# Two more second-layer products in quarters, their ends summed in PSUM

## The chip, the cores and the metric

The kernel runs on one core of a Trainium2 chip. The metric is the device time of one execution in microseconds (us), as a median over runs.

## The reference

Everything is f32. Four layers follow one another; the change lies in the third, and in the second layer's feed-forward part, which shares its code.

```python
x = _L0_cond_ref(x, A_grid, B_grid, dt)        # finite differences on a 512x512 grid, cut to 8 batches in the kernel
# _L1: attention block, then
h = _ln(x) * g2 + beta2                        # x: (8, 512, 512) in the kernel
ff = _gelu2(h @ W1 + b1) @ W2 + b2             # W1: 512x2048, W2: 2048x512
x = x + ff
# _L2: an expert of 8 is chosen for each batch
h = gelu(x @ Wi[e] + bi[e])                    # Wi: 512x2048
o = h @ Wo[e] + bo[e]                          # Wo: 2048x512
r = o + x
y = (r - mean(r)) * rsqrt(var(r) + 1e-12) * gamma[e] + beta[e]
# _L3: a gate from the mean over the rows, and a low-rank response
x = y + strength * (((y @ basis) @ basis.T[:, :R]) @ resp_w.T + resp_b + safety_bias)
```

## The kernel before

The grid stage and the attention stage fill the first 1079 us and are not touched. Then `mlp_stage` runs sixteen **phases** q = 0 to 15, one per batch and layer: q = 0 to 7 are the feed-forward part of _L1 for the 8 batches, q = 8 to 15 the expert layer of _L2. Phases 9 to 15 also finish the batch of the phase before (`tail_norm`, `tail_normed`, `tail_gamma`, `tail_feats`, `gate`, `strength`, `add_beta`, `tail_sum`, `tail_add`: the layer norm and _L3), and phases 0 to 7 also hold the Gram-Schmidt steps (`gs_norm`, `gs_b`) for _L3's basis.

One phase multiplies 512x512 by 512x2048 (first layer) and 512x2048 by 2048x512 (second layer). Both products are done with seven instead of eight half-size products (Winograd's form of Strassen's scheme, in which sums S of the left operand and T of the right one are formed first, and the seven results are added up):

- First layer: in four column groups g = 0 to 3, seven products each (list `L1`), of four matmuls 128x128 by 128x256. The left sums S come from the weights `wi` (`w_quads`, on GpSimd, written POOL), the right sums T from the normalised and transposed input b (`b_quads`, on VectorE, written DVE). Tiles u in PSUM hold the products, DVE adds them up into `act`, and ScalarE (ACT) applies gelu in place.
- Second layer: seven products p1, p5, p2, p6, p3, p7, p4 in this order. `second` computes one as 16 matmuls of 128x256 into one PSUM tile y. `third` computes one as again seven quarter products of 128x128 blocks (28 matmuls of 128x128, with sums by `quarters`), into two PSUM tiles "a" and "b" that DVE adds up in an SBUF tile w. p7 and p4 use `third`; p1, p5, p2, p6 and p3 use `second`. In phase 15, p4 is done in two halves (`last_row`), so that the end of the run is short.

The order is written out by hand. `pin` keeps every instruction in program order on its engine, and the work of the other engines is placed by **steps** (hooks): `at(hooks, s, f)` runs f before step s of the phase. Steps 0 to 27 are the first layer's products, 28 to 31 p1, 32 to 35 p5, 36 to 39 p2, 40 to 43 p6, 44 to 47 p3, 48 to 51 p7, 52 to 55 p4; a step is a product of the first layer, a column group of a second-layer product, or seven quarter matmuls.

Names that the change and the prediction use:

- `add` (line 1217) is a two-operand DVE instruction, `gadd` (line 1220) one on POOL, `mm` (line 1211) a matmul. `stage` (line 1569) copies an operand to PSUM by ScalarE, in one of two buffers ("tr"), so that a DVE sum has one operand in PSUM and one in SBUF. Products live in six PSUM buffers ("u").
- `t13`, `t2s2`, `t4s4`, `s13`: the sums T1, T3, T2, T4 (POOL) and S1, S3, S2, S4 (DVE) of the second layer.
- `x_add` adds a product into one quadrant of x; `yu` holds a sum of p1 and p6.
- `rows32` transposes blocks of the next phase's input, `turn` and `spread` send them through DRAM to the transposed tile bt; `scale` (phases 0 to 6) applies g2 and beta2 to it.
- `load_wi(q, g)` loads 1 MB of weights into buffer x0 to x3 (tag `x{g}`). Buffers x1 to x3 of a phase serve the sums of the quarter products once its weights are used; x0 does not.
- `load_extra` loads the expert's bias, gamma and beta rows. DMAs are issued on SyncE's queue (SP).

Of the kernel before, what the change touches and what calls it, by code (L numbers as in the profile page):

```python
# [20 lines left out]
NB = 8  # L21
# [1176 lines left out]
def mlp_stage(tc, a, small, xp, io, wo8, x1d, ident, eidx, sigs, layernorm, rstd_of, phalf, wl3, g2, b1, first):  # L1198
# [4 lines left out]
    with ExitStack() as ctx:  # L1203
# [293 lines left out]

        def b_quads(q, hold=False):
            def b(i, k, j):
                v = bts[q][2 * i + k]  # L1500
                return v[:, 2 * j : 2 * j + 2, :, :] if len(v.shape) == 4 else v[:, H * j : H * j + H]

            t1, t2, t4 = (
                as_rows(ap.tile([P, 2, H], F32, name=f"tb{i}_{q}", tag=f"tb{i}", bufs=1), b(0, 0, 0))
                for i in range(3)
            )
            for k in range(2):
                add(t1[k], b(0, k, 1), b(0, k, 0), ALU.subtract)
                add(t2[k], b(1, k, 1), t1[k], ALU.subtract)

            def rest():
                for k in range(2):
                    add(b(0, k, 1), b(1, k, 1), b(0, k, 1), ALU.subtract)
                for k in range(2):
                    add(t4[k], b(1, k, 0), t2[k], ALU.subtract)

            if not hold:
                rest()
            tbs[q] = {
                "B00": lambda k: b(0, k, 0), "B10": lambda k: b(1, k, 0),  # L1520
                "B11": lambda k: b(1, k, 1), "T3": lambda k: b(0, k, 1),
                "T1": lambda k: t1[k], "T2": lambda k: t2[k],
                "T4": lambda k: t4[k],
            }
            return rest
# [26 lines left out]
        def run(q, hooks):  # L1552
# [13 lines left out]
            def stage(key, src):  # L1566

                t = ps.tile([P, src.shape[1], src.shape[2]], F32, name=f"st_{q}_{key}", tag="tr")
                pin(nc.scalar.copy(t, src))  # L1569
                st[key] = t  # L1570
# [3 lines left out]
            def s13(g):  # L1574
                t = st.pop(f"s13_{g}")
                ss[g] = io.tile([P, 2, H], F32, name=f"s_{q}_{g}", tag=f"v{g}", bufs=2)
                add(ss[g], t, act_quad(g, 1, 1))
                add(act_quad(g, 1, 0), act_quad(g, 0, 0), t, ALU.subtract)

# [52 lines left out]
            wo, ts = wos[q], {}  # L1632
            tvs = extra["t", q]

            def second(s, A, B, each=None):
                y = ps.tile([P, 2, H], F32, name=f"y_{q}_{s}", tag="u", bufs=6)
                for g in range(NG):
                    go(s + g)
                    if s == 28 and g == 1:
                        stage(f"s13_{NG - 1}", act_quad(NG - 1, 1, 0))  # L1640
                    if s == 28 and g == 2:
                        s13(NG - 1)
                    for i in range(2):
                        for m in range(2):
                            mm(
                                y[:, m, :], A(g)[:, i, m * P : (m + 1) * P], B(g)[:, i, :],
                                g + i + m == 0, g + i + m == NG + 1,
                            )
                    if each:
                        each(g)  # L1650
                return y

            def quarters(key, i, j, wi_, wj, homes):


                def left(k, m):
                    o = H * i + P * m
                    return acts[:, :, 2 * j + k, o : o + P]

                def right(k, n):  # L1660
                    o = H * wj + P * n
                    return wo[:, :, 2 * wi_ + k, o : o + P]

                s1, s2, s4, t1, t2, t4 = homes
                L, M = left, right
                four[key] = dict(
                    a=((L(0, 0), M(0, 0)), (s2, t2), (L(0, 1), M(0, 1)), (s1, t1)),
                    b=((L(1, 0), M(1, 0)), (s4, M(1, 1)), (L(1, 1), t4)),
                )
                sub = ALU.subtract  # L1670
                of_left = [
                    lambda: (stage(key + "a", L(0, 1)), stage(key + "b", L(0, 0))),
                    lambda: (
                        add(s1, st[key + "a"], L(1, 1)),
                        add(L(0, 1), L(0, 0), st[key + "a"], sub),
                        stage(key + "c", L(1, 0)),
                    ),
                    lambda: (add(s2, s1, st[key + "b"], sub), add(s4, st[key + "c"], s2, sub)),
                ]
                of_right = [  # L1680
                    lambda: gadd(t1, M(0, 1), M(0, 0), sub), lambda: gadd(M(0, 1), M(1, 1), M(0, 1), sub),
                    lambda: gadd(t2, M(1, 1), t1, sub), lambda: gadd(t4, M(1, 0), t2, sub),
                ]
                return of_left, of_right

            four = {}
            homes = {}

            def quarter_homes(n):
                for k in range(1, 4)[n:]:  # L1690
                    t = xp.tile([P, KC, D], F32, name=f"q4_{q}_{k}", tag=f"x{k}", bufs=1)
                    homes[k] = [t[:, c, :].rearrange("p (g d) -> p g d", g=NG) for c in range(KC)]

            def third(s, key):

                jobs = [
                    (n, k, g, v) for n in "ab" for k, v in enumerate(four[key][n]) for g in range(NG)
                ]
# [4 lines left out]
                y = ys["a"]  # L1703
                for i, (n, k, g, (A, B)) in enumerate(jobs):
                    if i % 7 == 0:
                        go(s + i // 7)
                    last = len(four[key][n]) - 1
# [9 lines left out]
                add(w[:, 0:3, :], ys["b"][:, 0:3, :], w[:, 0:3, :])  # L1717
                return w.rearrange("p (m n) d -> p m (n d)", m=2)

            def early_quarters():  # L1720
                quarter_homes(0)
                h1, h2, h3 = (homes[k] for k in (1, 2, 3))
                return (
                    quarters("p7", 1, 0, 0, 1, (h1[3], h2[0], h2[1], h1[0], h1[1], h1[2]))
                    + quarters("p4", 1, 1, 1, 0, (h3[1], h3[2], h3[3], h2[2], h2[3], h3[0]))
                )
# [10 lines left out]
            def t2s2(g):  # L1737
                if g < NG - 1:
                    stage(f"s2_{g + 1}", act_quad(g + 1, 0, 0))
                else:  # L1740
                    stage("s4_0", act_quad(0, 0, 1))
                gadd(tvs[g], quad(wo[:, g], 1, 1), tvs[g], ALU.subtract)
                add(ss[g], ss[g], st[f"s2_{g}"], ALU.subtract)

            def t4s4(g):
                if g < NG - 1:
                    stage(f"s4_{g + 1}", act_quad(g + 1, 0, 1))
                gadd(quad(wo[:, g], 1, 0), quad(wo[:, g], 1, 0), tvs[g], ALU.subtract)
                add(act_quad(g, 0, 1), st[f"s4_{g}"], ss[g], ALU.subtract)

            l7, r7, l4, r4 = early_quarters()
            for i, f in enumerate(r7):
                at(hooks, 28 + i, f)
            for i, f in enumerate(l7):
                at(hooks, 40 + i, f)
            if q < NQ - 1:
                for i, f in enumerate(l4):
                    at(hooks, 43 + 2 * i, f)
                for i, f in enumerate(r4):
                    at(hooks, 41 + i if q <= NB else 40, f)  # L1760
# [4 lines left out]
            p5 = second(32, lambda g: ss[g], lambda g: tvs[g], t2s2)  # L1765
            x_add(1, 1, p5)
            x_add(0, 1, p5)
            p2 = second(36, lambda g: act_quad(g, 0, 1), b(1, 0), t4s4)
            x_add(0, 0, p2)
            p6 = second(40, lambda g: ss[g], lambda g: tvs[g])  # L1770
            add(yu, p6, yu)
            x_add(0, 1, yu)
            p3 = second(44, lambda g: act_quad(g, 0, 1), b(1, 1))
            x_add(0, 1, p3)
            p7 = third(48, "p7")
            add(yu, p7, yu)
            x_add(1, 1, yu)
            x_add(1, 0, yu)
# [3 lines left out]
            else:  # L1782
                for m in range(2):
                    y = ps.tile([P, H], F32, name=f"y_{q}_52_{m}", tag="u", bufs=6)
                    for g in range(NG):
                        if g % 2 == 0:
                            go(52 + 2 * m + g // 2)
                        for i in range(2):
                            mm(
                                y, act_quad(g, 1, 1)[:, i, m * P : (m + 1) * P],  # L1790
                                b(1, 0)(g)[:, i, :], g + i == 0, g + i == NG,
                            )
                    last_row(m, y)

        def t13(q, g):
# [4 lines left out]
            extra.setdefault(("t", q), {})[g] = t  # L1800
# [23 lines left out]
        def tail_normed(q):  # L1824
            v, (mv, rs) = stats.pop(q)
            for r in range(len(v)):
# [6 lines left out]
        def tail_gamma(q, rows):  # L1833
            gamma = extra[q][1][1]
            m = xs[q][:, rows[0] : rows[-1] + 1, :]
            pin(
# [204 lines left out]
        for q in range(NQ):  # L2041
# [8 lines left out]
            if nx:  # L2050
# [3 lines left out]
                at(hooks, 21, load_wi, nx, 0)  # L2054
# [9 lines left out]
            if nx:  # L2064
# [11 lines left out]
                at(hooks, 51, b_quads, nx)  # L2076
                at(hooks, 46, w_quads, nx, 0, gadd)
            if q < NB:
                for i, s in enumerate((11 if q else 18, 25, 44, 51)):
# [9 lines left out]
            elif q > NB:  # L2089
# [14 lines left out]
                for r in range(R):  # L2104
                    at(hooks, 45, tail_sum, o, r)
# [96 lines left out]
```

## Time and profile before

| | |
|---|---|
| median of 3 runs | 2652.83 us (2650.5 to 2656.63) |
| profiled execution | 2656.1 us, its span 2654.3 us |
| granted TensorE clock | 0.995 |
| PE busy | 2609.9 us, 98% |
| DVE, POOL, ACT busy | 1950.1 (73%), 1598.1 (60%), 1177.3 (44%) us |
| the sixteen phases | from 1079 to 2654 us; phases 1 to 7 take 95.4 us each, phases 9 to 14 99.0 |

PE is TensorE's matmuls, PEld its weight loads, SPq SyncE's queue. A line Lnnn is a line of the kernel; `add`, `gadd` and `mm` are helpers, so many different instructions share lines 1217, 1220 and 1211, and the names of the tiles tell them apart. An f32 matmul appears as two rows of the trace.

### The profile page before, as it was taken

The numbers are of one execution on the slowest core, as the hardware profiler recorded it, in microseconds if no ns is written. First come the engines' busy times: TensorE is split into PE (matmuls) and PEld (weight loads), VectorE is DVE, ScalarE is ACT, GpSimd is POOL, SyncE is SP. The second block draws the span as 40 slices with busy tenths as digits, with TensorE's granted clock in tenths as the row PEclk, the third lists the DMA queues.
The fourth block names the chain that finished last, engine by engine and source line by source line (L and its number), as shares of the span: only waits on it lengthen the run. The fifth ranks groups of instructions, "written<-read, shape, count | busy, mean of one in ns | idle before, by whom it ended". The sixth has DMA issues, their size and how long they took to land.

```text
span 2654.3 us, 41760 instructions
## 1 busy us (share of the span) xinstructions
PE 2609.9 (98%) x14896; PEld 1954.8 (74%) x14896; DVE 1950.1 (73%) x3684; ACT 1177.3 (44%) x2416; POOL 1598.1 (60%) x1223
## 2 busy tenths in 40 slices
PE   6999999999999999999999999999999999999998
PEld 3455555555555555798899899898898898898897
DVE  7978798888888756577667667667567777776765
ACT  2576767776777766233233323321312422322322
POOL 3555665655555655477666766766665665666662
PEclk9999999999999999999999999999999999999999
DMA  9765756666766555552662563455245355255241
GB/s 322 253 227 187 258 195 240 215 237 207 248 227 227 170 186 170 158 165 68 167 195 53 150 196 96 127 167 166 93 147 188 98 183 195 91 187 197 86 154 41
DMA packets 241828, 460.46 MB, mean 173 GB/s; under 512 B 33904, under 2 KB 77496, under 8 KB 232534
## 3 DMA queue, kind: packets, MB, share of 16 engines
q1 hardware_dynamic: 237754, 447.04, 49.0%
q0 software_dynamic: 3552, 10.72, 4.3%
q8 instruction: 119, 1.95, 0.3%
q14 instruction: 87, 0.71, 0.1%
q10 hardware_dynamic: 316, 0.03, 0.0%
HBM read 398.43 MB, written 55.09 MB: 171 GB/s over the span
## 4 chain that ended last, share of the span: by engine, by line
PE 93%; DMA 2%; DVE 2%; ACT 1%; issue 1%; POOL 0%; SPq 0%; DVEq 0%; POOLq 0%; ACTq 0%
PE u L1211 28%; PE y L1211 21%; PE tr L564 8%; PE s L561 5%; PE ctx L561 4%; PE pv L561 4%; PE o L561 4%; PE pk L561 4%; PE pq L561 4%; PE y_48a L1211 2%; PE y_52a L1211 2%; PE y_48b L1211 2%; PE y_52b L1211 1%; PE l L253 1%; PE xb L564 1%
## 5 line engine op out<-in xcount | busy, mean ns | idle before, releaser
L998 POOL TENSOR_TENSOR bt<-bt,mk 128x1024 f32<-128x1024 f32 x256 | 542.0, 2142 | 59.3 <-DMA bt<-in_bias 49.4
L1026 ACT ACTIVATE bt<-bt,mn 128x512 f32<-128x512 f32 x512 | 365.8, 718 | 77.9 <-DVE mn L1021 77.6
L1211 PE MATMUL y<-wo,act 128*128 128x256 f32 x1568 | 352.2, 380 | 0.0
L564 PEld LDWEIGHTS tr<-ident,bt 128*128 128x128 f32 x2048 | 229.9, 142 | 150.3 <-issue 101.8
L1021 DVE CUSTOM_DVE_ANT_0 bt<-s,bt 128x512 f32<-128x512 f32 x512 | 329.9, 684 | 5.1 <-PE s L561 4.4
L1211 PE MATMUL u<-bt,wi 128*128 128x256 f32 x1440 | 330.5, 379 | 0.0
L1217 DVE TENSOR_TENSOR act<-u,u 128x512 f32<-128x512 f32 x256 | 174.1, 685 | 212.4 <-PE u L1211 155.1
L1211 PEld LDWEIGHTS y<-wo,act 128*128 128x128 f32 x1568 | 296.0, 190 | 46.2 <-issue 6.7
L1052 ACT COPY pt<-tr 128x512 f32<-128x512 f32 x376 | 207.8, 584 | 207.2 <-PE tr L564 199.8
L1211 PEld LDWEIGHTS u<-bt,wi 128*128 128x128 f32 x1440 | 272.4, 190 | 36.4
L564 PE MATMUL tr<-ident,bt 128*128 128x128 f32 x2048 | 277.0, 278 | 8.2 <-ACT pt L1052 3.5
L1211 PE MATMUL u<-tb,ws 128*128 128x256 f32 x1024 | 242.3, 379 | 1.3 <-DVE yw L1217 1.3
L1211 PE MATMUL y<-t,s 128*128 128x256 f32 x1024 | 227.8, 380 | 0.0
L1211 PEld LDWEIGHTS u<-tb,ws 128*128 128x128 f32 x1024 | 194.2, 190 | 28.2 <-issue 1.6
L1211 PEld LDWEIGHTS y<-t,s 128*128 128x128 f32 x1024 | 194.0, 190 | 26.1
L1590 ACT ACTIVATE act<-act,b 128x512 f32<-128x512 f32 x128 | 85.3, 714 | 271.9 <-DVE act L1217 207.4
L1050 DVE COPY pt<-tr 128x512 f32<-128x512 f32 x136 | 93.8, 689 | 134.0 <-PE tr L564 133.2
L1220 POOL TENSOR_TENSOR t<-wo,t 128x512 f32<-128x512 f32 x64 | 81.4, 1278 | 147.1 <-PE y L1211 147.1
L561 PE MATMUL s<-kt,qt 32*128 32x512 f32 x1024 | 165.9, 643 | 1.2 <-ACT kt L651 0.8
L1590 ACT ACTIVATE act<-act,bi 128x512 f32<-128x512 f32 x128 | 82.9, 711 | 188.1 <-DVE act L1217 188.0
L1217 DVE TENSOR_TENSOR u<-u,u 128x512 f32<-128x512 f32 x192 | 131.0, 682 | 42.7 <-PE u L1211 41.6
L1569 ACT COPY st_s<-act 128x512 f32<-128x512 f32 x192 | 111.9, 589 | 86.3 <-DVE act L1217 53.5
(378 smaller groups left out, 4852.4 us busy)
## 6 DMA issues: line engine op xcount, KB each, us to landing
bt<-in_bias SPq DMA_DIRECT2D x256, 512.0 KB
wo<-in_W SPq DMA_DIRECT2D x32, 1024.0 KB
wi<-in_Wi SPq DMA_DIRECT2D x32, 1024.0 KB
wo<-in_Wo_e SPq DMA_DIRECT2D x32, 1024.0 KB
wi<-in_W SPq DMA_DIRECT2D x28, 1024.0 KB
td<-tt SPq DMA_DIRECT2D x22, 1024.0 KB
bt<-td SPq DMA_DIRECT2D x176, 128.0 KB
gq<-coef_q SPq DMA_DIRECT2D x21, 512.0 KB
```

The source lines that it names most:

```text
L561: pin(nc.tensor.matmul(out, lhsT=lhsT, rhs=rhs, start=start, stop=stop))
L564: pin(nc.tensor.transpose(out, src, ident))
L998: nc.gpsimd.tensor_tensor(bt, bt, mask[b, r][:, None, :].to_broadcast([P, 2, S]), ALU.add)
L1021: nc.vector.tensor_tensor_reduce(bt[:, i, :], ss[h], bt[:, i, :], -1.0, 3.0e38, ALU.add, ALU.min, mn)
L1026: nc.scalar.activation(bt[:, i, :], bt[:, i, :], AF.Exp, bias=mn, scale=-1.0, accum_out=sums[b, c][:, h, r : r + 1],)
L1050: pin(nc.vector.tensor_copy(pt[:, :, r % 2, :], tr))
L1052: pin(nc.scalar.copy(pt[:, :, r % 2, :], tr))
L1211: pin(nc.tensor.matmul(out, lhsT=lhsT, rhs=rhs, start=start, stop=stop))
L1217: pin(nc.vector.tensor_tensor(out, x, y, op))
L1220: pin(nc.gpsimd.tensor_tensor(out, x, y, op))
L1569: pin(nc.scalar.copy(t, src))
L1590: nc.scalar.activation(acts[:, g, k, :], acts[:, g, k, :], func, bias=bi[:, j : j + 1])
```

## The change

1. p2 and p3 are computed by `third` too: four of seven second-layer products in quarters (in phase 15, where p4 stays in halves, three). Their sums are formed at new steps, by `l_sum` (ScalarE copies and DVE) and `r_sum` (POOL), in the buffers x0 to x3, which `set_up` hands out, and for p3's left sums in the buffers of s and t. p7 now comes before p3, except in phase 15.
2. Ends in PSUM: `third` adds the parts up in the PSUM tile "b" instead of the SBUF tile w, p6 and p7 are added to yu in PSUM, and x_add reads them there.
3. T4 and S4 of the halves go to the quadrants (0,0) of wo and act, which p1 has used, instead of (1,0) and (0,1).
4. `b_staged` replaces `b_quads` from the second phase on: the same eight sums, with one operand copied to PSUM by ScalarE.
5. In the tail of phases 9 to 15, gamma is copied to PSUM by ScalarE before the multiplication, and the normalisation moves from DVE to ScalarE.
6. Steps: the load of the next phase's wi 0 from 21 to 48, its sums from 46 to 51, the Gram-Schmidt step from 44 to 46, tail_sum from 45 to 46, the staging for s13(3) one step later.

```diff
+        def staged(key, *parts):
+
+            if len(parts) == 1:
+                t = ps.tile(list(parts[0].shape), F32, name=f"st_{key}", tag="tr")
+                pin(nc.scalar.copy(t, parts[0]))
+                return t
+            t = ps.tile([P, 2, H], F32, name=f"st_{key}", tag="tr")
+            halves = as_rows(t, parts[0])
+            for o, v in zip(halves, parts):
+                pin(nc.scalar.copy(o, v))
+            return halves
+
+        def b_staged(q):
...
+            b01, b11 = (staged(f"b{i}1_{q}", b(i, 0, 1), b(i, 1, 1)) for i in range(2))
+            for k in range(2):
+                add(t1[k], b01[k], b(0, k, 0), ALU.subtract)
+            for k in range(2):
+                add(t2[k], b11[k], t1[k], ALU.subtract)
+            for k in range(2):
+                add(b(0, k, 1), b11[k], b(0, k, 1), ALU.subtract)
...
+            b10 = staged(f"b10_{q}", b(1, 0, 0), b(1, 1, 0))
+
+            def rest():
+                for k in range(2):
+                    add(t4[k], b10[k], t2[k], ALU.subtract)
...
+            PLACES = {
+                "p2": ((0, 1), (1, 0)), "p7": ((1, 0), (0, 1)), "p3": ((0, 0), (1, 1)),
+                "p4": ((1, 1), (0, 0)),
+            }
...
+            def r_sum(key, n):
+                t1, t2, t3, t4 = rt[key]
+                if n == 0:
+                    gadd(t1, right(key, 0, 1), right(key, 0, 0), sub)
+                elif n == 1:
+                    gadd(t3, right(key, 1, 1), right(key, 0, 1), sub)
+                elif n == 2:
+                    gadd(t2, right(key, 1, 1), t1, sub)
+                else:
+                    gadd(t4, right(key, 1, 0), t2, sub)
+
+            def l_sum(key, n):
+                s1, s2, s3, s4 = lt[key]
+                if n == 0:
+                    stage(key + "a", left(key, 0, 1))
+                    stage(key + "b", left(key, 0, 0))
+                elif n == 1:
+                    add(s1, st[key + "a"], left(key, 1, 1))
+                    add(s3, left(key, 0, 0), st[key + "a"], sub)
+                    stage(key + "c", left(key, 1, 0))
+                else:
+                    add(s2, s1, st[key + "b"], sub)
+                    add(s4, st[key + "c"], s2, sub)
+
+            def set_up(part):
+                if part == 0:
+                    fresh(2)
+                    r_homes("p2", *hx[2])
+                elif part == 1:
+                    fresh(0, 1, 3)
+                    l_homes("p2", *hx[3])
+                    r_homes("p7", *hx[0][0:3])
+                    r_homes("p3", *hx[1][0:3])
+                elif part == 2:
+                    fresh(2, 3)
+                    l_homes("p7", hx[0][3], hx[1][3], hx[2][0])
+                    r_homes("p4", *hx[2][1:4])
+                    l_homes("p3" if last else "p4", *hx[3][0:3])
...
+            def t4s4(g):
...
+                gadd(quad(wo[:, g], 0, 0), quad(wo[:, g], 1, 0), ts[q, g], ALU.subtract)
+                add(act_quad(g, 0, 0), st[f"s4_{g}"], ss[g], ALU.subtract)
+
+            tail, last = q > NB, q == NQ - 1
+            four = (40, 41, 42), (44, 45, 46)
+            for part, s in enumerate((25, 28, 40, 44)):
+                at(hooks, s, set_up, part)
+            for key, ss_, ts_ in (
+                ("p2", (28, 29, 30), (25, 26, 27, 28)),
+                ("p7", four[last], (29, 30, 31, 31)),
+                ("p3", four[not last], (40, 40, 40, 40) if tail else (40, 41, 42, 43)),
+                ("p4", (47, 48, 49), (44, 44, 44, 44) if tail else (43, 44, 45, 46)),
+            ):
...
-                add(w[:, 0:3, :], ys["b"][:, 0:3, :], w[:, 0:3, :])
-                return w.rearrange("p (m n) d -> p m (n d)", m=2)
+                y = ys["b"]
+                pin(nc.scalar.copy(y[:, 3, :], w[:, 3, :]))
+                add(y[:, 0:3, :], y[:, 0:3, :], w[:, 0:3, :])
+                return y.rearrange("p (m n) d -> p m (n d)", m=2)
...
-            p2 = second(36, lambda g: act_quad(g, 0, 1), b(1, 0), t4s4)
+            p2 = third(36, "p2")
             x_add(0, 0, p2)
-            p6 = second(40, lambda g: ss[g], lambda g: tvs[g])
-            add(yu, p6, yu)
-            x_add(0, 1, yu)
-            p3 = second(44, lambda g: act_quad(g, 0, 1), b(1, 1))
-            x_add(0, 1, p3)
-            p7 = third(48, "p7")
-            add(yu, p7, yu)
-            x_add(1, 1, yu)
-            x_add(1, 0, yu)
+            p6 = second(40, lambda g: ss[g], lambda g: ts[q, g])
+            add(p6, p6, yu)
+            x_add(0, 1, p6)
+            pin(nc.scalar.copy(yu, p6))
+            for s, key in zip((44, 48), ("p3", "p7") if last else ("p7", "p3")):
+                p = third(s, key)
+                if key == "p3":
+                    x_add(0, 1, p)
+                else:
+                    add(p, p, yu)
+                    x_add(1, 1, p)
+                    x_add(1, 0, p)
...
         def tail_normed(q):
             v, (mv, rs) = stats.pop(q)
+            if q < NQ - 1:
...
+                        nc.scalar.activation(
+                            v[r], v[r], AF.Identity, bias=sh[:, r : r + 1], scale=rs[:, r : r + 1]
+                        )
...
         def tail_gamma(q, rows):
             gamma = extra[q][1][1]
             m = xs[q][:, rows[0] : rows[-1] + 1, :]
+            if q < NQ - 1:
+                gamma = staged(f"gamma_{q}", gamma)
...
-                at(hooks, 21, load_wi, nx, 0)
+                at(hooks, 48, load_wi, nx, 0)
...
-                at(hooks, 51, b_quads, nx)
-                at(hooks, 46, w_quads, nx, 0, gadd)
+                at(hooks, 51, b_staged, nx)
+                at(hooks, 51, w_quads, nx, 0, gadd)
             if q < NB:
-                for i, s in enumerate((11 if q else 18, 25, 44, 51)):
+                for i, s in enumerate((11 if q else 18, 25, 46, 51)):
...
-                    at(hooks, 45, tail_sum, o, r)
+                    at(hooks, 46, tail_sum, o, r)
```

## The prediction

> **What bounds the kernel now.** I read the page's busy table first, then the chain that ended last, then the waits of PE, and last the other engines phase by phase. About 0.2% (5 us) is what a measurement of this kernel can tell from no change.
>
> ```profile
> PE 2609.9 (98%) x14896; PEld 1954.8 (74%) x14896; DVE 1950.1 (73%) x3684; ACT 1177.3 (44%) x2416; POOL 1598.1 (60%) x1223
> ```
>
> PE is busy 98% of the span. The chain in order of time (start, us, what) gives one whole phase of the sixteen, here phase 1:
>
> ```profile
> 1175.01 48.35 PE u L1211 x224
> 1223.36 34.53 PE y L1211 x160
> 1257.89 3.57 PE y_48a L1211 x32
> 1261.46 2.68 PE y_48b L1211 x24
> 1264.14 3.57 PE y_52a L1211 x32
> 1267.71 2.68 PE y_52b L1211 x24
> 1270.39 48.35 PE u L1211 x224
> ```
>
> Each stretch begins where the last one ends: PE never waits in the 95.38 us. A matmul of f32 shows as two rows, so a product of 16 half-size matmuls (32 rows) takes 34.53/5 = 6.906 us, and a product already in quarters, 28 matmuls (56 rows), takes 3.57 + 2.68 = 6.25 us. The mean of one row (380 and 275 ns) overstates both, because matmuls overlap; the spacing counts. In the waits of PE from 1080 us on, one wait exceeds 1 us:
>
> ```profile
> PE u L1211 <- DVE yw L1217: 1.3, 1, 1.3
> ```
>
> So work taken off PE shortens the run, provided that the other engines keep up. Their load by phase (phase 2, then phase 10, which also finishes the batch before it):
>
> ```profile
> core 0: us, PE busy (x) PEld busy (x) DVE busy (x) ACT busy (x) POOL busy (x), PEclk, DMA share, GB/s
> ...
> 1270.40:1365.80 95.40, 95.40 (x497) 85.48 (x497) 65.98 (x131) 29.62 (x49) 64.37 (x54) 1.00 0.50 138
> ...
> 2041.70:2140.70 99.00, 99.00 (x548) 87.56 (x547) 70.42 (x110) 29.77 (x52) 61.79 (x43) 1.00 0.47 157
> ```
>
> **PE's part of the change.** p2 and p3 become quarter products in all 16 phases: 32 times 6.906 - 6.25 = 0.656 us, together 21.0 us off PE. Shapes, operands' types and order of the quarter matmuls are those of p7 and p4, whose spacing is 223 ns each in every phase; I take it unchanged. [...]
>
> **What feeds PE.** Per phase the two new quarter products add:
> - POOL: 8 sums of 128x512 at 1.27 us = 10.2 us. 64.4 becomes 74.6 of about 94.1 us; in the later phases 62 becomes 72 of 97.7.
> - DVE: 8 sums at 0.68 = 5.4 us, and two endings of 0.29 + 0.29 + 0.42 + 0.55 = 1.55 us each: 8.5 us. Against it, the additions into x and yu take an operand from PSUM. The two kinds stand in the groups by shape:
>
> ```profile
> L1217 DVE TENSOR_TENSOR x<-yu,x 128x512 f32<-128x512 f32 x48 | 56.2, 1198 | 1.1
> L1217 DVE TENSOR_TENSOR x<-y,x 128x512 f32<-128x512 f32 x80 | 53.4, 683 | 62.9 <-ACT yu L1762 55.6 <-PE y L1211 7.3
> ```
>
> With both operands in SBUF one takes 1.2 us on average (up to 4.14 beside POOL's 4.52 us addition of beta), with one in PSUM 0.68. Three per phase save 1.5 us, the fourth (x<-yw,x, 1377 ns) 0.7. DVE goes from 66 to about 72 us of 94. In phases 9 to 14 it also loses the four normalisations at 1.27 (5.1 us, to ScalarE) and about 1 us of gamma's multiplication (3.30 us; 2.29 where POOL was idle): 70 stays 70.
> - ScalarE: 6 copies at 0.59, one more of yu at 0.58, two at 0.27, four more at 0.27 for the ends in PSUM, six of 128x256 for b (between 0.27 and 0.59): 8 us. 30 becomes 38; later phases also get four normalisations at 0.80 and gamma's copy. None of this is near the end of a phase's 94 us.
>
> No row shows DVE writing PSUM. The bounds are 0.55 us for the 128x384 ending (PSUM in, SBUF out) and 0.9 (the contended 1.2 us of 512 columns, scaled); below the first nothing suggests a gain, since ScalarE's copies take 0.59 into PSUM and 0.58 into SBUF. I take 0.55: one operand still comes from PSUM.
>
> **Is it in time?** Steps are 1.73 us of PE, in quarter products 1.56.
> - p2: POOL's sums at steps 25 to 28, DVE's at 28 to 30, needed at step 36. In between lie 13.8 us of p1 and p5, and DVE idles 3.5 us there in one wait (x<-y <- yu). Covered; if not, p2 would wait for its second group.
> - p7, p3, p4: POOL's order is t2s2, T4, p3's four, p4's four. T4 no longer overwrites what p2 reads, so POOL need not wait for PE there (13 us of waits in phases 1 to 7). From p5's end it needs 12 x 1.28 = 15.4 us to the end of p4's sums; p4 starts 25.7 us after p5.
> - The load of the next phase's wi 0 moves from step 21 to 48, behind load_extra and the spread on SP's queue but ahead of the output stores; its four sums from step 46 to 51, behind the Gram-Schmidt power and ahead of the next one. The load can start when p7 ends. From the issue of such a load (wi 1) to POOL's first sum the timelines have 5.7 us (2035.49 to 2041.16) and 7.8 (2134.47 to 2142.28), and the chain 6.7 (from 1836.60), which I take. S2 is then ready 6.7 + 2.6 = 9.3 us after p7; it is needed at 12.5 (two quarter products) + 3.45 (two u products) = 15.95. Covered by 6.6 us, and at 7.8 still by 5.5.
> - This adds one wait: in phases 0 to 7 the power of gs_norm at step 51 now queues behind those four sums, and DVE's gs_b (step 53) waits for the power, with p4's ending and the next act sums queued behind it. Load 6.7, sums 5.5, power 1.0, gs_b 1.5 to 3.3, first half of the ending 1.0: 15.7 to 17.5 us after p7. PE wants that PSUM buffer back at 12.5 + 6.9 = 19.4. Covered by 2 to 4 us, with a load of 7.8 us by 1 at least.
> - b's sums: the same eight, 0.42 each, behind six ScalarE copies; T2 is wanted at the 15.95 above, and they start 4.7 us after p7 at the earliest. Cost nothing.
> - Phases 9 to 14, steps 36 to 41: DVE's queue is full there. In the timeline of phase 10:
>
> ```profile
> 2107.60 3.30 DVE L1837 TENSOR_TENSOR x<-x,gamma 128x2048 f32<-128x2048 f32 x1
> ...
> 2112.22 0.20 DVE L1900 TENSOR_SCALAR h<-pg,gb 128x1 f32<-128x1 f32 x1
> ...
> 2114.44 0.28 PE L1211 MATMUL pz<-h,gw 128*128 128x1 f32 x2
> ```
>
> pz stands in PE's order and needs h. Counted from p2's start (2103.7): DVE is free of p5's additions at 2.2; then two transposes 1.4, three T4/S4 sums 2.0, gamma 2.3, ft 0.3, p2's first ending 1.0, h 0.35 make 9.55, and waits for the two staging buffers some 0.8: 10.4. PE reaches pz at 6.25 + 1.0 (pf) + 0.8 (pg) + 1.73 = 9.8. So PE would wait 0.6 us in six phases: 3.6 us, between 0 and 9.6 (gamma still at 3.30). Next late is p7's s2, which came 5.0 us after pz began and is wanted 6.2 after it; I take nothing.
> - Phase 15: the norm of its first rows follows p3, whose sums now end with 0.55 + 0.68 instead of 0.68, while PE reaches the transposes sooner; the 0.6 us wait there grows by about 0.8.
> - Phase 8: the 1.3 us wait above stood behind DVE additions of 3.33 and 3.25 us (x<-yu, x<-yw) beside POOL's; those get PSUM operands, so it goes.
>
> Sum on the profiled execution (2656.1 us): -21.0 - 1.3 + 3.6 + 0.8 = -17.9, thus 2638.2. It stood 3.3 us above the median of 2652.83; off the median: **2635 us**.
>
> **Rivals.**
> - *No change: DVE sets the end of the seven last phases.* If gamma stays at 3.30 (1.6 us wait for pz) and the multiplication by sigs stays at the 1.10 us it took in phase 10 beside POOL, so that s2 is about 1 us late, each of seven phases loses 2.6 us: 18. -21.0 - 1.3 + 18 + 0.8 = -3.5: 2649. For it: DVE has no idle time over 0.5 us between 2104 and 2112. Against: gamma and x take PSUM operands.
> - *Slower: the moved load.* Place: DVE's gs_b behind POOL's sums behind wi 0, and S2 itself. It decides from a load of about 10.3 us (19.4 less 5.5, 1.0, 1.5 and 1.0). At 12.5 us each of 15 phases loses 2.2 us: 33 - 22.3 = +11 and more, 2665. Against: loads of this size took 5.7 to 7.8 us; for: up to four such loads now stand close together.
> [...]
>
> **Numbers.** Forecast 0.74; DVE bound 0.16 (0.05 of it still faster by over 0.2%, 0.09 same, 0.02 slower); moved load 0.09; spacing 0.01. Faster 0.79, same 0.09, slower 0.12. The range runs from -22.3 with a little more from DVE's lighter additions (2629) to the DVE rival (2650), which leaves out 0.1.
>
> **What would show it.** PE: 768 more matmul rows (15664); phase 1's chain: u 48.35, then y x96 at 20.7, and four quarter pairs of 6.25, a phase of 94.07 us. Phases 9 to 14 at 97.7 plus PE's wait for h, seen as pz waiting for DVE. POOL about 75 us per phase. x additions at 0.68. Wrong if y_36 or y_44 is spaced over 223 ns, if PE waits for POOL's ws or for u's buffers at a phase's start, or if a wait above 1 us per phase appears in phases 1 to 7.

## The result, and the profile after

The changed kernel takes 2649.02 us (median; 2644.45 to 2652.66) against 2653.64 us before: a ratio of 0.9983, 95% interval 0.9977 to 0.999. The forecast was 2635. Of the 17.9 us that it promised, 4.6 came.

The profiled execution has a span of 2646.5 us. The page's busy line shows the 768 matmul rows more that were foreseen (15664), and PE busy 16 us less:

```profile
PE 2593.9 (98%) x15664; PEld 1968.5 (74%) x15664; DVE 1993.3 (75%) x3919; ACT 1311.1 (50%) x2748; POOL 1733.2 (65%) x1351
```

The length of each phase, from its first matmul to the next phase's (the last one to the end of the span), tells more than the span, because the untouched stages ahead end anywhere between 1072.8 and 1079.7 us in the profiles of this study:

| us | phase 0 | 1 to 7, each | 8 | 9 to 14, each | 15 | all sixteen |
|---|---|---|---|---|---|---|
| before | 95.8 | 95.39 | 100.0 | 98.98 | 117.9 | 1575.3 |
| after | 102.4 | 94.97 | 98.8 | 97.67 | 119.7 | 1571.8 |
| forecast's steps | 94.5 | 94.08 | 97.4 | 98.3 | 117.3 | 1557.4 |

Phases 9 to 14 lost 1.31 us each, which is two products at 0.656. Phases 1 to 7 lost a third of that, and phases 0 and 15 grew. The waits of PE from 1070 us on (engine, line, tile, what it waited for: total us, times, longest) name the places:

```profile
PE y_52a L1211 <- DVE q L1217: 6.2, 8, 1.6
PE y L1211 <- ACT act L1740: 2.6, 1, 2.6
PE u L1211 <- DVE yw L1217: 1.8, 1, 1.8
PE ytr L1214 <- DVE x L1934: 1.5, 1, 1.5
PE y_44a L1211 <- DVE q L1217: 1.2, 1, 1.2
```

Before, there was one wait above 1 us. Now DVE is late for the second group of p4 (y_52a) in phases 0 to 7, for the first products of phase 8 (u), for phase 15's transposes (ytr, of the normalised rows), and in phase 0 for the last gelu (ACT act, which waited for DVE) and p7 (y_44a).

**Phases 1 to 7.** The longer pieces of the chain in order of time (start, us, what), from p1 to p4 of phase 2 of the changed kernel:

```profile
1320.70 13.81 PE y L1211 x64
1334.51 3.57 PE y_36a L1211 x32
1338.08 2.68 PE y_36b L1211 x24
1340.76 6.92 PE y L1211 x32
1347.71 0.71 DVE y L1217
1348.44 0.70 DVE x L1217
1356.25 0.71 DVE y_44b L1217
1356.98 1.29 DVE x L1217 x2
1359.04 0.74 DVE qm L1277
1361.72 2.92 PE y_52a L1211 x24
```

The quarters have the foreseen spacing (p2: 3.57 + 2.68 = 6.25 us). But the chain leaves PE behind p6 and comes back to it only in p4: between them DVE's queue sets the time. In DVE's timeline of that stretch (start, us, engine, line, operation, out<-in, and in brackets its idle time and what ended it):

```profile
1350.35 0.69 DVE L1217 TENSOR_TENSOR s<-st_p3a,act 128x512 f32<-128x512 f32 x1 [1.22 <-ACT st_p3a L1502]
...
1351.56 0.68 DVE L1236 CUSTOM_DVE_ANT_0 junk_gn<-qb 64x512 f32<-64x512 f32 x1
...
1355.65 0.57 DVE L1217 TENSOR_TENSOR y_44b<-y_44b,yw 128x384 f32<-128x384 f32 x1 [0.39 <-ACT y_44b L1834]
...
1358.19 0.14 DVE L1250 TENSOR_SCALAR gs_d<-gs_d 64x1 f32<-64x1 f32 x1
...
1359.71 0.68 DVE L1217 TENSOR_TENSOR q<-st_p4a,act 128x512 f32<-128x512 f32 x1
1360.31 0.67 DVE L1217 TENSOR_TENSOR act<-act,st_p4a 128x512 f32<-128x512 f32 x1
1360.90 0.67 DVE L1217 TENSOR_TENSOR q<-q,st_p4b 128x512 f32<-128x512 f32 x1
```

The third Gram-Schmidt step (norm at step 46: 1351.56 to 1352.78; gs_b at step 48: 1358.19 to 1359.71) is 2.7 us of DVE time right ahead of p4's sums. The third of these (q<-q,st_p4b), on which y_52a's second group waits, ends at 1361.6, and PE goes on at 1361.72. Its wait is 0.65 us; counted by the whole phase, PE loses 94.97 - 94.08 = 0.89 us.

**Phase 0.** POOL's timeline, then DVE's:

```profile
1122.19 1.27 POOL L1220 TENSOR_TENSOR q<-wo 128x512 f32<-128x512 f32 x1
1123.43 4.51 POOL L1220 TENSOR_TENSOR x<-x,b2row 128x2048 f32<-128x2048 f32 x1
1127.90 1.25 POOL L1220 TENSOR_TENSOR q<-wo 128x512 f32<-128x512 f32 x1
```

```profile
1124.17 5.01 DVE L1276 TENSOR_TENSOR al<-al,below 64x1 f32<-64x1 f32 x1
```

al multiplies 64 numbers, both operands in SBUF; in phase 2 it takes 0.15 us. Here it begins 0.7 us after the add of b2's row (`add_row`) and ends with the POOL operation behind that, at 1129.2. p2's first sum on POOL (q, 1122.19) has put add_row just where DVE reaches al. Behind al the last act additions and the gelu are late, and PE waits 2.6 us. The windows of PE around that wait (length, PE busy, granted clock, DMA):

```profile
core 0: us, PE busy (x), PEclk, DMA share, GB/s
1124.00:1128.50 4.50, 4.50 (x23) 1.00 0.00 0
1128.50:1131.30 2.80, 0.29 (x2) 0.99 0.00 0
1131.30:1134.70 3.40, 3.34 (x8) 0.51 1.19 39
1134.70:1140.00 5.30, 5.30 (x27) 1.00 0.00 0
```

For 3.4 us after the wait PE runs at half clock (granted 0.51): another 1.7 us, an estimate (half of the 3.34 us that PE is busy there).

**Phase 8.** The wait at its start was to go; it grew. POOL's timeline, then DVE's:

```profile
1834.90 1.04 POOL L1259 DMA_DIRECT2D qb<-qm  x2 [5.55 <-DVE qm L1277]
```

```profile
1843.61 0.68 DVE L1236 CUSTOM_DVE_ANT_0 junk_gn<-qb 64x512 f32<-64x512 f32 x1 [2.78 <-DMA qb<-qm]
...
1849.61 0.60 DVE L1217 TENSOR_TENSOR yw<-y_52a,yw 128x128 f32<-128x128 f32 x2
```

gs_b at 48 ends by having POOL send qm back as qb. That DMA is issued at 1834.90, and DVE, at the end of b's sums, stands idle for it for 2.78 us, until 1843.61, with p4's ending, which frees PE's PSUM buffer, queued behind. At the start of phases 2 to 7 the same step waits 1.4 to 1.7 us for its qb, and no wait of PE follows.

**Phase 15.** The transposes wait 1.53 us for the normalised rows, against 0.6 before. In this execution the clock fell behind that wait too:

```profile
2612.00:2617.00 5.00, 4.81 (x44) 1.00 0.25 105
2617.00:2619.50 2.50, 1.03 (x7) 0.99 0.00 0
2619.50:2622.90 3.40, 3.40 (x16) 0.50 0.40 158
```

### The profile page after: what moved, and what is told of

Its sections match the earlier page's. It is cut to its first block, busy times and chain, and to the rows that moved or that the text cites. A ratio compares the mean times of both kernels' runs of the same rounds, so it can differ in the third digit from the quotient of the medians.

```text
span 2646.5 us, 44047 instructions
## 1 busy us (share of the span) xinstructions
PE 2593.9 (98%) x15664; PEld 1968.5 (74%) x15664; DVE 1993.3 (75%) x3919; ACT 1311.1 (50%) x2748; POOL 1733.2 (65%) x1351
## 4 chain that ended last, share of the span: by engine, by line
PE 88%; DVE 7%; DMA 3%; issue 1%; ACT 1%; SPq 0%; POOL 0%; DVEq 0%; POOLq 0%; ACTq 0%
PE u L1211 28%; PE y L1211 12%; PE tr L564 8%; PE s L561 5%; PE ctx L561 4%; PE pv L561 4%; PE o L561 4%; PE pk L561 4%; PE pq L561 4%; PE y_36a L1211 2%; PE y_52a L1211 2%; PE y_36b L1211 2%; PE y_52b L1211 1%; PE y_44a L1211 1%; PE y_48a L1211 1%
## 5 line engine op out<-in xcount | busy, mean ns | idle before, releaser
L1220 POOL TENSOR_TENSOR q<-wo,q 128x512 f32<-128x512 f32 x126 | 160.6, 1274 | 4.4
L1220 POOL TENSOR_TENSOR wo<-wo 128x512 f32<-128x512 f32 x111 | 141.1, 1271 | 8.7
```

Source lines behind the costliest of these rows:

```text
L1220: pin(nc.gpsimd.tensor_tensor(out, x, y, op))
```

## The experiments

The theory after the result: the quarters bring their 21 us, and DVE is late at three places that the forecast held for covered: phase 0 (al beside add_row), phases 1 to 8 (the third Gram-Schmidt step), phase 15 (its first norm). Rivals: the moved load of wi 0; DVE's load as a whole, so that p2's quarters bring nothing; DVE as the limit of the last phases. Ratios are against the kernel before; that of the changed kernel is 0.9983. All other edits are to the changed kernel.

**e1_row_early**

```diff
-            at(hooks, 2 if q else 26, add_row, q)
+            at(hooks, 2 if q else 17, add_row, q)
```

> Edit: in phase 0 alone POOL's add of b2's row to x (4.5 us) goes from step 26 to step 17, ahead of the second-layer weight sums, where POOL stood idle for 4.4 us. My theory (lateness in phase 0): VectorE's al at 1124.2 us (5.01 us, through two POOL operations) falls to under 0.5 us, TensorE's 2.6 us wait for the last gelu of the first layer and the stretch of granted clock 0.52 behind it go, and phase 0 falls from 102.4 us to between 96.5 and 98.5 us (the constants of step 38 still hold VectorE back later); the time falls by 4 to 6 us against the changed kernel, to about 2644. Rival (the moved load of wi 0, or POOL's longer queue, is what costs): nothing changes, phase 0 stays within 1 us of 102.4 and the time within 1 us of 2649. Phases 1 to 15 stay as they are by both.

2643.78 us, ratio 0.996 (0.9947 to 0.9973). al takes 0.53 us (at 1123.90), PE's wait for gelu and the half clock are gone, and phase 0 is 97.1 us; phases 1 to 14 stay within 0.02 us. So one place in POOL's queue cost 5.3 us, and neither the load nor POOL's longer queue did.

**e2_gs_early**

```diff
-                for i, s in enumerate((11 if q else 18, 25, 46, 51)):
+                for i, s in enumerate((11, 18, 25, 51)):
```

> Edit: the Gram-Schmidt step of 46/48 goes into the first layer in phases 0 to 7 (steps 11/13, 18/20, 25/27, 51/53). My theory (VectorE's queue in steps 44 to 52 is full in phases 0 to 7): the wait of TensorE for p4's sums (y_52a behind VectorE's q, 0.8 us in each) goes, phases 1 to 7 fall from 94.97 to between 94.0 and 94.3 us, phase 0 by 1 to 2 us, the time by 6 to 8 us against the changed kernel, to about 2642. Rival (the wait is ScalarE's copies or POOL's right-hand sums, and VectorE's q only shows last): phases 1 to 7 stay above 94.7 us and the time falls by under 2 us. Phases 8 to 15 stay as they are by both.

2644.47 us, ratio 0.9967 (0.9955 to 0.998). Phases 1 to 7 are 94.08 us each, the forecast's value, and the wait at y_52a is gone: 0.89 x 7 = 6.2 us. Phase 8 falls by 2.0 us, which was not expected: qb is now sent in time. Phase 0 grew to 104.0 us instead of falling, since al met add_row again (4.99 us) and PE waited 6.2 us for gelu.

**e3_turn_late**

```diff
-                    at(hooks, (51, 52, 53, 53)[c], tail_turn, q, half, [c])
+                    at(hooks, (52, 53, 54, 55)[c], tail_turn, q, half, [c])
```

> Edit: in phase 15 the transposes of the first two rows go from steps 51, 52, 53, 53 to 52, 53, 54, 55. My theory (TensorE waits 1.5 us for the normalised rows at step 51, and its granted clock falls behind that wait): the wait is under 0.3 us, the clock between 2618 and 2624 us of the trace is back at 1.0, phase 15 falls from 119.5 to between 116.5 and 118 us, the time by 1.5 to 3 us against the changed kernel. Rival (the clock falls there for another reason, and the tail is only moved later): phase 15 stays above 118.8 us, the time within 0.7 us.

2645.89 us, ratio 0.9974 (0.9964 to 0.9984); the interval overlaps that of the changed kernel, so that the phases say more than the time. The wait for the rows is gone and no fall of the clock stands there; phase 15 is 115.5 us, 4.3 less and more than expected. Not all of it is the edit's. Nine profiled kernels have the steps of the changed kernel's phase 15 (one of them with p2 in halves, one with its ends in SBUF). All nine have the wait, of 1.2 to 1.5 us; in three (the changed one, where it was 0.50 for 3.4 us, e1, e7) the clock fell behind it, and they show 119.6 to 119.7, the other six (e9 among them, with 1.00 at that place) 117.6 to 119.3. In the three profiles below the clock also falls to 0.50 shortly before the end and stays there, from a different place in each. PE in that last stretch (us, PE busy, granted clock, DMA), in the kernel before, the changed one and e3:

```profile
2646.20:2654.30 8.10, 1.50 (x8) 0.50 0.32 129
2636.50:2646.50 10.00, 3.11 (x14) 0.50 0.26 105
2634.20:2641.40 7.20, 0.65 (x4) 0.50 0.35 146
```

At half clock, half of PE's busy time is lost (an estimate): 0.8, 1.6 and 0.3 us. The 4.3 us are then the wait's 1.5, 1.7 for the 3.4 us at half clock behind it, which hits some executions and not others, and 1.2 at the end, which the edit did not cause as far as the runs show: 4.4 in all.

**e4_three**: the edits of e1, e2 and e3 together.

> Edit: the edits of e1_row_early, e2_gs_early and e3_turn_late together. If the three losses are what the forecast missed, they add: 11 to 17 us under the changed kernel, about 2632 to 2638, and phases 0, 1 to 7 and 15 at about 96, 94.2 and 117.5 us. If TensorE is paced by something else behind them, the sum is under 8 us.

2641.68 us, ratio 0.9956 (0.9944 to 0.9968): 7 us under the changed kernel, not 11 to 17. Phases 1 to 14 are those of e2, phase 15 is 117.8, but phase 0 is 103.9. DVE's timeline in phase 0:

```profile
1112.47 4.53 DVE L1236 CUSTOM_DVE_ANT_0 junk_gn<-qb 64x512 f32<-64x512 f32 x1 [1.36 <-DMA qb<-qm]
```

and POOL's:

```profile
1111.94 4.51 POOL L1220 TENSOR_TENSOR x<-x,b2row 128x2048 f32<-128x2048 f32 x1
```

With the Gram-Schmidt step at 11, POOL waits for it, the work behind it on POOL comes 9 us later than in e1, counted from the phase's start, and add_row meets the next norm (junk_gn). The collision had been moved, not removed.

**e5_placed**

```diff
-            at(hooks, 2 if q else 26, add_row, q)
+            at(hooks, 2 if q else 17, add_row, q)
...
-                for i, s in enumerate((11 if q else 18, 25, 46, 51)):
+                for i, s in enumerate((11, 18, 25, 51) if q else (18, 25, 38, 51)):
...
-                at(hooks, 38, constants)
+                at(hooks, 21, constants)
...
-                    at(hooks, (51, 52, 53, 53)[c], tail_turn, q, half, [c])
+                    at(hooks, (52, 53, 54, 55)[c], tail_turn, q, half, [c])
```

> Edit: the placements of e1_row_early and e3_turn_late, the Gram-Schmidt steps of e2_gs_early in phases 1 to 7 alone, and in phase 0, where e2_gs_early and e4_three ran into POOL's work, the third one at 38/40 and the constants at step 21 instead of 38. All arithmetic as in the changed kernel. If lateness of VectorE at three places is all that the forecast missed, phase 0 is 94.5 to 96.5 us, phases 1 to 7 are 94.1, phase 8 is 96.8, phases 9 to 14 are 97.7 and phase 15 is 115.5 to 117.8, the time 15 to 19 us under the changed kernel, about 2630 to 2634, which is what the forecast promised. Rival (a loss that is still unseen comes back elsewhere): the phases do not add up to that, and the gain over the changed kernel stays under 10 us.

2630.91 us (2628.52 to 2631.95), ratio 0.9917 (0.9903 to 0.9931). Phases: 95.8, seven of 94.08, 96.8, six of 97.67, 116.7; 1553.9 in all, 17.8 under the changed kernel. This is the fastest version, ahead of both kernels, with the same arithmetic as the changed one. Its chain in order of time has what the forecast wrote for a phase, PE without a break:

```profile
1168.81 48.35 PE u L1211 x224
1217.16 13.81 PE y L1211 x64
1230.97 3.57 PE y_36a L1211 x32
1234.55 2.68 PE y_36b L1211 x24
1237.23 6.91 PE y L1211 x32
1244.13 3.57 PE y_44a L1211 x32
1247.71 2.68 PE y_44b L1211 x24
1250.39 3.57 PE y_48a L1211 x32
1253.96 2.68 PE y_48b L1211 x24
1256.64 3.57 PE y_52a L1211 x32
1260.21 2.68 PE y_52b L1211 x24
```

One wait above 1 us is left, y_44a in phase 0 (1.1 us), behind the Gram-Schmidt step that now stands at 38.

**e6_p2_halves**

```diff
-                ("p2", (28, 29, 30), (25, 26, 27, 28)),
...
-            p2 = third(36, "p2")
+            p2 = second(36, lambda g: act_quad(g, 0, 1), b(1, 0))
```

> Edit: p2 alone is made as a product of halves again (64 matmuls), without its sums; everything else as in the changed kernel. If a quartered product is worth 0.66 us of TensorE's time (6.91 - 6.25) wherever nothing is late, phases 1 to 8 and 9 to 14 grow by 0.65 each (to 95.6 and 98.3 us), and VectorE's q is still late for p4 in phases 1 to 7. Phase 0 falls from 102.4 to between 98.5 and 100.5 us, since the first sum of p2 on POOL no longer stands ahead of the add of b2's row and al is held by that alone. In all 5 to 8 us slower than the changed kernel. Rival (a quartered product brings nothing, since VectorE's sums for p2 push everything behind them): phases 1 to 7 stay at or under 95.0 us and the time within 2 us or below.

2654.19 us, ratio 1.0004 (0.9994 to 1.0014): 5.6 us slower than the changed kernel by the ratios. Phases 1 to 7 and 9 to 14 grow by 0.65 us each (one by 0.88), the wait at y_52a stays at 6.2 us in eight phases, and phase 0 falls to 98.4 (al 2.57 us, as in the kernel before). A quartered product is worth its 0.656 us wherever nothing is late, and the lateness in phases 1 to 7 does not come from p2's sums.

**e7_norm_gamma_dve**

```diff
             v, (mv, rs) = stats.pop(q)
-            if q < NQ - 1:
+            if False:
...
-            if q < NQ - 1:
+            if False:
                 gamma = staged(f"gamma_{q}", gamma)
```

> Edit: in phases 9 to 14 the tail's normalisation is VectorE's again and gamma is read from SBUF by VectorE, as in the kernel before (some 5 and 1 us more of VectorE's time in each of these phases). If VectorE has room there, the seven phases 9 to 15 stay within 0.3 us of 97.67 and the time within 2 us of the changed kernel. Rival (VectorE sets the end of the last phases): phases 9 to 14 grow by 1 us or more each, the time by 6 us or more.

2649.1 us, ratio 0.9984 (0.9975 to 0.9993); phases 9 to 14 stay at 97.67 us. DVE has room there, and this part of the change brought nothing that the time shows. gamma itself took 2.27 us from SBUF in this order (3.30 before, the median of its eight), which suggests that it was POOL's work beside it that had made it long.

**e8_b_sums_sbuf**

```diff
-                at(hooks, 51, b_staged, nx)
+                at(hooks, 51, b_quads, nx)
```

> Edit: b's sums at step 51 are made from SBUF by VectorE as in the kernel before, without ScalarE's copies to PSUM; POOL's sums of the first-layer weights stay at step 51 beside them. If VectorE's operations with both operands in SBUF wait for POOL's (as al did in phase 0), the sums go from 0.41 us to 0.6 us or more each, TensorE waits at the start of the next first layer, and phases 0 to 14 grow by 0.5 us or more each: 7 us or more slower. Rival (the copies to PSUM bring nothing, al in phase 0 was a case by itself): the sums stay near 0.41 us, the phases within 0.1 us, the time within 2 us of the changed kernel.

2672.64 us, ratio 1.0072 (1.0057 to 1.0088): 24 us slower than the changed kernel, as the first theory had it (7 us or more), but not in the phases that it named. b's sums in the groups by shape:

```profile
L1217 DVE TENSOR_TENSOR tb<-bt,tb 128x256 f32<-128x256 f32 x60 | 56.9, 969 | 1.0
L1217 DVE TENSOR_TENSOR tb<-bt 128x256 f32<-128x256 f32 x30 | 32.2, 1072 | 0.0
```

With operands in PSUM these took 414 and 415 ns on average, and 422 and 416 from SBUF in the kernel before, where POOL's sums stood at another step. Yet phases 0 to 8 hardly change, since the longer sums are covered there. Phases 10, 11, 13 and 14 take 102.3 to 103.1 us, phase 12 98.8: in these the last `tail_add` and p3's ending stand behind the sums, and PE waits for them at the next phase's start:

```profile
PE u L1211 <- DVE x L2038: 13.9, 5, 3.7
```

In phases 10, 11, 13 and 14, where this wait is 2.9 to 3.7 us, the clock record shows 3.4 us at half clock behind it, some 1.7 us of PE's time each (the estimate used under e3); in phase 12, where it is 0.85 us, none. 13.9 + 4 x 1.7 = 20.7 of the 20.9 us by which these five phases grew. The copies to PSUM are therefore needed, because w_quads now runs on POOL at the same step.

**e9_gs_44**

```diff
-                for i, s in enumerate((11 if q else 18, 25, 46, 51)):
+                for i, s in enumerate((11 if q else 18, 25, 44, 51)):
```

> Edit: the third Gram-Schmidt step back at 44/46, where the kernel before has it; all else as in the changed kernel. In phase 2 of the changed kernel VectorE stood idle for 1.15 and 1.22 us in steps 43 to 45, ahead of the step at 46/48. If it is the late place of these 2.8 us that holds p4's sums back, they fall into that idle time, phases 1 to 7 fall from 94.97 to between 94.1 and 94.5 us and the time by 3 to 6 us. Rival (VectorE's queue is full from step 44 on wherever they stand): the wait stays, before y_52a or now before y_48a (p3's sums), and phases 1 to 7 stay above 94.8 us, the time within 1.5 us.

2641.4 us, ratio 0.9948 (0.9932 to 0.9965). Phases 1 to 7 are 94.57 us, just over what was expected of the first theory, and the time fell by 7.6 us, more than the 3 to 6 expected, since phase 8 and phase 15 were not in that sum: 0.4 us of the 0.89 comes from the place at 46/48, and 0.5 stays, 0.16 us of it within p3's first tile and 0.33 within p4's. Phase 8 is 96.8, without its wait. So both hold in part: the move 44 to 46 cost 0.4 x 7 + 2.0 = 4.8 us in phases 1 to 8, and DVE's queue is too full for this step at 44 and 46 too; other places between 44 and 52 were not run. (Phase 15 was 118.0 here, 1.7 us less: the wait is there, the fall behind it is not.)

**e10_ends_sbuf**

```diff
-                y = ys["b"]
-                pin(nc.scalar.copy(y[:, 3, :], w[:, 3, :]))
-                add(y[:, 0:3, :], y[:, 0:3, :], w[:, 0:3, :])
-                return y.rearrange("p (m n) d -> p m (n d)", m=2)
+                y = ys["b"]
+                add(w[:, 0:3, :], y[:, 0:3, :], w[:, 0:3, :])
+                return w.rearrange("p (m n) d -> p m (n d)", m=2)
```

> Edit: the ends of the quartered products p2, p7, p3 and p4 are summed in SBUF as in the kernel before (ScalarE's copy of the fourth quarter goes too), so the adds to x and yu have both operands in SBUF. If VectorE's queue is what limits steps 44 to 52 of phases 0 to 7, these adds grow from 0.69 us to 1.0 us or more, p4's sums come later still, and phases 1 to 7 grow from 94.97 to between 95.6 and 97 us: 5 us or more slower than the changed kernel. Phases 9 to 14, where VectorE had room, grow by less than 0.5 us each. Rival (the ends in PSUM are worth nothing): the phases stay within 0.2 us and the time within 1.5 us.

2647.08 us, ratio 0.9973 (0.9961 to 0.9986). This expectation was wrong in sign: five of phases 1 to 7 are 94.67 us, 0.3 shorter, and two 94.96 and 95.03. The adds from SBUF are longer on average (968 ns, against 686 to 692 from PSUM in the changed kernel), but not at the place that counts, where POOL is idle (for 5.28 us, it waits for qm). The group of phases 1 to 7, then the timeline at p7's end in phase 2:

```profile
L1217 DVE TENSOR_TENSOR x<-yw,x 128x512 f32<-128x512 f32 x36 | 34.3, 968 | 1.0
```

```profile
1361.72 1.29 DVE L1217 TENSOR_TENSOR x<-yw,x 128x512 f32<-128x512 f32 x2
```

Two adds in 1.29 us are the 1.29 of the changed kernel's adds from PSUM, while DVE's idle 0.39 us for ScalarE's copy of the fourth quarter (y_44b, in the timeline above) is gone. Phase 0 grows from 102.4 to 104.1, but that does not show that the ends in PSUM pay there: the clock was at half for 6.8 us in this execution instead of 3.4, with PE busy for 5.9 of them, which alone is 1.3 us or so more.

**e11_load_50**

```diff
-                at(hooks, 48, load_wi, nx, 0)
+                at(hooks, 50, load_wi, nx, 0)
```

> Edit: the load of wi 0 for the next phase goes from step 48 to step 50, some 3.5 us later. The forecast held that it has 6.6 us of cover before the first sum on it. If so nothing moves: phases 0 to 14 within 0.2 us, the time within 1.5 us of the changed kernel. Rival (the load decides when the next first layer starts): phases 1 to 14 grow by 1 us or more each, the time by 10 us or more.

2648.38 us, ratio 0.9983 (0.9972 to 0.9994). Phases 0 to 7 and 9 to 14 stay within 0.05 us; phase 8 is 97.9 instead of 98.8. The load keeps its cover when it starts two steps later.

**e12_placed_p2_halves**: e5_placed with the edit of e6_p2_halves.

> Edit: e5_placed with p2 alone as a product of halves again, as in e6_p2_halves. With nothing late, a quartered product is worth 0.66 us in each of the 16 phases: phases 1 to 8 grow from 94.08 and 96.81 to 94.7 and 97.5, phases 9 to 14 from 97.67 to 98.3, the time by 9 to 11 us over e5_placed, to about 2641. Rival (part of what e5_placed won is VectorE's or POOL's work for p2 that its placements hid, so that without it the phases get shorter elsewhere): less than 6 us.

2642.76 us, ratio 0.9953 (0.9936 to 0.9969): 0.0036 above e5_placed, 9.6 us. Phases 1 to 7 are 94.73 and 9 to 14 98.32, 0.65 more each; phase 0 is 95.1, 0.8 less, because without p2's sums DVE is in time for y_44a.

## Why the prediction was wrong, step by step

| step of the forecast | forecast | in the phases after | shown by |
|---|---|---|---|
| 32 quartered products | -21.0 | -21.0 | -1.31 in each of phases 9 to 14; 0.65 per product in e6, e12; e5's chain |
| phases 1 to 7, covered | 0 | +6.2 | e2: gone; e9: 2.8 of it by the move to 46 |
| phase 0, covered | 0 | +7.9 | e1: 5.3 by add_row; 6.6 in e5 |
| phase 8's wait | -1.3 | +0.1 | e2, e9: -2.0 |
| PE waits for h (pz) | +3.6 | 0 | after: no such wait in phases 9 to 14 |
| phase 15's transposes | +0.8 | +3.2 | the wait 0.9, the clock some 2.5 (under e3) |
| sum | -17.9 | -3.6 | |

- **PE's part** was right: 6.25 us per quartered product (y_36 and y_44, 3.57 + 2.68 each in e5's chain: 223 ns a matmul, 0.517 of the 432 ns of twice the columns), and 94.08 us for a phase in which nothing is late.
- **"Is it in time?", p2, p7, p3, p4** is the step that failed. For p7, p3 and p4 it counted POOL's queue, and DVE's only in phases 9 to 14. In phases 0 to 7 DVE has the Gram-Schmidt steps instead of the tail, and they were never put into the queue between p6 and p4. The change moves one of them from 44 to 46, and this was not costed at all: its 2.7 us of DVE time, and the DMA of qb that gs_b issues, which the next step waits for (phase 8).
- **Phase 0** was taken to be like phases 1 to 7. It alone has add_row in the first layer's end (step 26). The row that warned was there before, in DVE's timeline of phase 0:

```profile
1128.13 2.56 DVE L1276 TENSOR_TENSOR al<-al,below 64x1 f32<-64x1 f32 x1
```

- **Phase 8**: the additions of 3.3 us did become short, but the wait had a second cause in line, qb's DMA.
- **pz** (the gate's second matmul, which needs h from DVE) erred to the other side. h was ready 9.1 us after p2's start, not 10.4: the same DVE instructions follow one another a little faster than their rows last (sums of 0.68 us begin 0.6 apart), and the 0.8 us for staging buffers did not come. PE reached pz at 10.1, not 9.8.
- **Phase 15**: the wait grew by 0.9 as forecast (0.8); the clock was not in the sum. The 3.4 us at half clock behind the wait are some 1.7 us (the estimate under e3), and PE had 3.11 instead of 1.50 us of work in the last stretch at half clock, another 0.8: with the wait 3.4, of the 3.2 measured.
- **Rivals.** DVE as the limit of the last seven phases is refuted by e7; the moved load by e11. No run shows the wider spacing of quarter matmuls on which the forecast put 0.01: y_36 and y_44 take the 6.25 us of y_48 and y_52. The number near 2649 that the DVE rival gave was reached by another mechanism: DVE was the limit in the first nine phases. That 2649.02 lies inside the range, whose upper end this rival set, is therefore luck. The load rival's own terms give 19.4 - 9.0 = 10.4 us and not 10.3, and 2664 and not 2665; nothing hangs on it.
- **The ends in PSUM** were credited with shorter additions. e10 shows that this was so on average, but not at the place that set the time, where ScalarE's copy cost more than the adds gained.
- **The sign** that was to tell of lateness in phases 1 to 7, a wait above 1 us in each, was set too high: 0.65 us of wait, 0.89 of phase, cost 6.2 us.

What stays open: why the clock falls behind some waits of PE and not behind others of the same length, and what holds phase 0 of e5_placed 0.6 us above 94.08 + 1.1. Against phase 1, its products fall back by 0.3 us within the first three and by another 0.3 around the wait at y_44a; the cause is not shown.

## What to carry to other kernels

When an engine at 98% is relieved, make the second engine's queue, instruction by instruction, for every kind of phase, the first one included; the sum of its work in a phase (71 of 95 us here) says nothing about a stretch of 10 us in which it is nearly full. Cost every step that a change moves, with its DMAs, also those that have nothing to do with the arithmetic: here one hook from 44 to 46 and one POOL operation in the wrong place took back 4.8 + 5.3 us, more than half of the promised 17.9, and moving four hooks returned it. A tiny instruction that already lasted 2.56 us was here the sign of a collision that the change doubled, to 5.01 us. And before two single executions are compared, set aside what each lost at half clock: in e3 that was 2.9 of 4.3 us.

## What the runs showed of the hardware

- al, a DVE instruction with both operands in SBUF, took longer beside POOL's operations, and ended with one of them. In phase 2 it takes 0.15 us; in phase 0 it took 2.56 us beside add_row alone in the kernel before (both rows end at 1130.7) and 2.57 in e6, and 5.01 and 4.99 us where another POOL operation followed add_row at once (the changed kernel, e2). There al did not end with add_row, at 1127.9 and 1131.6, but with the second operation, at 1129.2 and 1132.8. The ends of these rows suggest that a DVE instruction that is already waiting can go on waiting through the next POOL operation.
- The granted clock halved for 3.4 us (in phase 0 of e10 for 6.8) behind some waits of PE, and not behind others. In the changed kernel a wait of 2.6 us (phase 0) was followed by 3.4 us at 0.51, and one of 1.5 us (phase 15) by 3.4 us at 0.50. Behind the same 1.5 us wait the clock of e9 stayed at 1.00. In e3 the wait for gelu in phase 0 (2.5 us) had no fall behind it (1.00 from 1131 to 1150 us), while the next one, 2.7 us at y_44a, had (0.83 on average from 1150 to 1160). In e2 6.2 us of waiting for gelu were followed by 0.50 on average from 1135 to 1140 us. Behind the waits of 0.65 us in phases 1 to 7 of the changed kernel there is none: the granted clock is 1.00 in each of these phases.
